# Mamba steps that take both channel halves at once: tiled gathers, 64-partition reads, and a step size summed on TensorE

## The chip, the cores and the metric

The kernel runs on one core of a Trainium2 chip. The metric is the device time of one launch in microseconds (us). The kernel before takes 8183.77 us, the median of three runs (8181.15 to 8186.65).

## The reference

Input is `x`, two images of 64 channels by 96 by 96 pixels, float32 throughout. Four layers follow each other.

```python
# layer 0: attention over the 9216 pixels of each image, then 1x1 conv, batch norm, residual
# layer 1: depthwise 3x1 and 1x3 + 1x1 conv + batch norm + relu, then one Mamba over the
#          9216 pixels of an image as ONE sequence, plus residual
# layer 2: four Mambas: forward and backward along the columns, then along the rows;
#          every row or column (96 long) is a sequence of its own
# layer 3: a dynamic 3x3 filter per channel group
def mamba(h):                                   # D_INNER = 128 channels d, 16 states s
    xm, z = split(h @ in_proj_w.T)
    xc = silu(causal_conv4(xm) + convd_b)
    dt, B, C = split(xc @ x_proj_w.T)           # 4, 16, 16
    dt = softplus(dt @ dt_proj_w.T + dt_proj_b) # per channel and pixel: the "step size"
    # for every channel d and state s, along the sequence t:
    #   hc = hc * exp(dt*A[d,s]) + dt * B[s] * xc[d];   y[d] = sum_s hc * C[s]
    return ((y + xc * Dp) * silu(z)) @ out_proj_w.T
```

The scan has 128 x 16 = 2048 independent rows (channel, state) for each pixel position, sixteen times the 128 partitions of the chip's memory.

## The kernel before, in words

Layer 0 (to about 2700 us of the profile) and layer 3 (the last 80 us) are not touched. The Mambas of layers 1 and 2 are run by the class `Mamba`, which is given a list of 120 *units*: 24 of layer 1 (`u.carry` is set: the scan goes on from the unit before), then 96 of layer 2 (`u.carry` is None). A unit is 768 pixels (`CH`), in two halves of 384 (`HALF`), and it takes 16 *steps*.

Per unit a prologue makes the channel values `xc`, the gate, the step size `dt` and the product `e = dt*xc`, each 128 channels by 768. `step_write` puts `dt` and `e`, together `u.both` of 128 x 1536, into a DRAM tile `rows` of 256 x 1536, twice, one copy under the other. Step n then reads 128 rows from row 8n on (`read`), so that partition p holds channel (p + 8n) mod 128; partition p always belongs to state p // 8. Over 16 steps each partition meets every channel that it has to. In layer 2 (`u.paired`) a step handles two such groups, 2m and 2m+1, over one half of the pixels, in two reads of 128 partitions by 3 KB; in layer 1 a step handles one group over all 768 pixels, in one read of 128 partitions by 6 KB.

A step is a chain over five engines: SyncE issues the read five steps ahead (`READ`); ScalarE makes exp(dt*A) three steps ahead (`decay`, L853 and L857); VectorE multiplies by B (`inputs`, L872 and L877, into a PSUM tile `place`) and scans (`scan`, L884 and L890); GpSimd multiplies the scanned `h` by C (L886 and L893); TensorE sums over the states with a permutation matrix of 128 x 128 (`gather`, L910), accumulating in a PSUM tile `low`. TensorE also makes B (`shared`, L866) and the prologue of later units (`mm`, L666; `conv`, L748 and L754).

The order is written out by hand: the table `PIECES` says at which step, counted from the unit's own first step, each prologue piece is issued, `lates` how many steps a gather lags its scan, and `run` issues all of it under a manual schedule, so every engine works through its queue in that order. SyncE issues every read and write of the steps, in one queue. The step size is log(1 + e^a) in parts: ScalarE writes `e`, `kept`, `log` and `dt`, and GpSimd adds them up in three full-width instructions (L805, L808, L811) before it multiplies by `xc` (L815).

Of the kernel before, what the change touches and what calls it, by code (L numbers as in the profile page):

```python
# [25 lines left out]
P = 128  # L26
# [497 lines left out]
def mamba_tables(k, pool):  # L524

    nc = k.nc
    G = P // 8
    t = SimpleNamespace()  # L530

    t.member = pool.tile([P, 8], FP, name="member")
    nc.vector.reduce_sum(t.member, k.ident.rearrange("p (g i) -> p i g", i=8), axis=AX.X)
    t.group = pool.tile([P, 2, G], FP, name="group")
    for j in range(2):
        nc.vector.reduce_sum(t.group[:, j], k.ident.rearrange("p (g i) -> p g i", i=8), axis=AX.X)

    t.turned = pool.tile([P, G, G], FP, name="turned")
    two = t.group.rearrange("p j g -> p (j g)")
    for n in range(G):  # L540
        nc.vector.tensor_copy(t.turned[:, n], two[:, G - n : 2 * G - n])

    pair = pool.tile([P, 2, P], FP, name="pair")
    nc.vector.tensor_copy(pair, k.ident.unsqueeze(1).to_broadcast([P, 2, P]))
    pair = pair.rearrange("p j c -> p (j c)")
    t.gather = [pair[:, P - 8 * n : 2 * P - 8 * n] for n in range(G)]

    t.centre = pool.tile([P, P], FP, name="centre")
    nc.vector.tensor_sub(t.centre, k.ident, k.mean_c)
    return t  # L550
# [8 lines left out]
def mamba_weights(k, w, pool, product, tables, i):  # L559
# [15 lines left out]
    p = product(tables.placed.rearrange("p s i -> p (s i)"), tables.group[:, 0], P, G)  # L575
# [38 lines left out]
class Mamba:  # L614
# [14 lines left out]

    STEPS = P // 8  # L630
# [3 lines left out]
    def __init__(self, k, tables, wk, dram, ps, ps_m):  # L634
        self.k, self.nc, self.t = k, k.nc, tables
        self.wk, self.dram, self.ps_m = wk, dram, ps_m


        self.places = [self.wide(ps.tile([P, 2 * NB], FP, name=f"place{i}")) for i in range(2)]
        self.low = [ps.tile([P, NB], FP, name=f"low{i}")[:, :HALF] for i in range(2)]  # L640
# [141 lines left out]
    def step_read(self, u):  # L782
# [3 lines left out]
        order = "p (j a t) -> p a j t" if u.paired else "p (a j t) -> p a j t"  # L786
        both = u.both.rearrange(order, a=2, j=2)
# [6 lines left out]
    def step_exp(self, u):  # L794
        nc = self.nc
        nc.scalar.activation(u.e, u.e, AF.Exp, scale=-1.0)
        nc.scalar.activation(u.kept, u.e, AF.Identity, bias=1.0)
        nc.scalar.activation(u.kept, u.kept, AF.Identity, bias=self.k.minus)  # L798
# [5 lines left out]
    def step_kept(self, u):  # L804
        self.nc.gpsimd.tensor_sub(u.kept, u.e, u.kept)  # L805

    def step_sum(self, u):
        self.nc.gpsimd.tensor_add(u.log, u.log, u.kept)  # L808

    def step_dt(self, u):  # L810
        self.nc.gpsimd.tensor_add(u.dt, u.dt, u.log)  # L811

    def step_u(self, u):
# [7 lines left out]
    def step_write(self, u):  # L821
        u.rows = self.dram.tile([2 * P, 2 * CH], FP, tag="rows", name="rows")
        for j in range(2):
            self.nc.sync.dma_start(out=u.rows[j * P : (j + 1) * P], in_=u.both)
# [10 lines left out]
    def paired(self, step):  # L835
        half, m = divmod(step, self.STEPS // 2)
        return half, (2 * m, 2 * m + 1)

    def read(self, u, step):
        u.dtu[step] = self.work("spread", 2 * CH, bufs=6)  # L840
        if not u.paired:
            self.nc.sync.dma_start(out=u.dtu[step], in_=u.rows[8 * step : 8 * step + P])
            return
        half, groups = self.paired(step)
        for q, n in enumerate(groups):
            row = u.rows[8 * n : 8 * n + P, bass.ts(half, CH)]
            self.nc.sync.dma_start(out=u.dtu[step][:, bass.ts(q, CH)], in_=row)

    def decay(self, u, step):

        h = u.h[step] = self.work("h", bufs=9)
        if not u.paired:
            self.nc.scalar.activation(h, u.dtu[step][:, :CH], AF.Exp, scale=u.w.rates[:, step : step + 1])  # L853
            return
        for q, n in enumerate(self.paired(step)[1]):
            dt = u.dtu[step][:, q * CH : q * CH + HALF]
            self.nc.scalar.activation(h[:, bass.ts(q, HALF)], dt, AF.Exp, scale=u.w.rates[:, n : n + 1])  # L857

    def shared(self, u, half=0):

        if u.paired:
            sides, halves = [self.low[0]], [half]
        else:
            (sides, u.B), halves = self.places[1], range(2)
        for j, p in zip(halves, sides):
            self.nc.tensor.matmul(p, lhsT=u.w.bc[0], rhs=u.xc[:, bass.ts(j, HALF)], start=True, stop=True)  # L866

    def inputs(self, u, step):

        if not u.paired:  # L870
            u.bx = self.places[0][1]
            self.nc.vector.tensor_mul(u.bx, u.dtu[step][:, CH:], u.B)  # L872
            return
        bx = self.places[step % 2][1].rearrange("p (q t) -> p q t", q=2)
        x = u.dtu[step].rearrange("p (q a t) -> p q a t", q=2, a=2)[:, :, 1]
        B = self.low[0].unsqueeze(1).to_broadcast([P, 2, HALF])
        self.nc.vector.tensor_mul(bx, x, B)  # L877

    def scan(self, u, step):
        nc = self.nc  # L880
        h = u.h[step]
        if not u.paired:
            first = u.carry[:, step : step + 1]
            nc.vector.tensor_tensor_scan(h, h, u.bx, first, ALU.mult, ALU.add)  # L884
            nc.gpsimd.tensor_copy(first, h[:, CH - 1 :])  # L885
            nc.gpsimd.tensor_mul(h, h, u.C)  # L886
            return
        bx = self.places[step % 2][1]
        way = slice(None, None, -1) if u.rev else slice(None)
        nc.vector.tensor_tensor_scan(h[:, way], h[:, way], bx[:, way], 0.0, ALU.mult, ALU.add)  # L890
        h = h.rearrange("p (q t) -> p q t", q=2)
        C = u.C[:, bass.ts(self.paired(step)[0], HALF)]
        nc.gpsimd.tensor_mul(h, h, C.unsqueeze(1).to_broadcast([P, 2, HALF]))  # L893

    def gather(self, u, step):

        if u.paired:
            half, groups = self.paired(step)
            parts = [(half, self.low[1], q, n) for q, n in enumerate(groups)]
            begin, end = step % 8 == 0, step % 8 == 7  # L900
        else:
            parts = [(j, p, j, step) for j, p in enumerate(self.low)]
            begin, end = step == 0, step == self.STEPS - 1
        h = u.h[step]
        if begin:
            for half, p in {half: p for half, p, _, _ in parts}.items():
                self.nc.tensor.matmul(p, lhsT=u.w.direct, rhs=u.xc[:, bass.ts(half, HALF)], start=True, stop=False)  # L907
        for i, (_, p, q, n) in enumerate(parts):
            stop = end and (i == 1 or not u.paired)
            self.nc.tensor.matmul(p, lhsT=self.t.gather[n], rhs=h[:, bass.ts(q, HALF)], start=False, stop=stop)  # L910

    def y_half(self, u):
        if u.paired:
            u.y = self.work("yg")
            self.nc.scalar.copy(u.y[:, :HALF], self.low[1])  # L915

    def y_read(self, u):
        if u.paired:
            self.nc.scalar.copy(u.y[:, HALF:], self.low[1])
        elif not u.drained:  # L920
            u.y = self.work("yg")
            for j, p in enumerate(self.low):
                self.nc.scalar.copy(u.y[:, bass.ts(j, HALF)], p)
# [20 lines left out]
    def tail_read(self, u):  # L944
# [25 lines left out]
        (-19, "step_read"),  # L970
        (-18, "step_exp"),
        (-17, "step_kept"),
        (-17, "step_log"),
        (-17, "c_mm"),
        (-15, "c_read"),
        (-15, "step_sum"),
        (-11, "step_dt"),
        (-9, "step_u"),
        (-8, "step_write"),
# [10 lines left out]
    def lates(now, s):  # L990
        halves = now and now[0].paired
        if s == 2 or (s == 10 and halves):
            return ()
        if s == 3 or (s == 11 and halves):
            return (3, 2)
        return (2,)

    def run(self, units, first, n_first, other):


        for u in units:
            u.dtu, u.h, u.paired, u.drained = {}, {}, not u.carry, False
        steps = [(u, s) for u in units for s in range(self.STEPS)]
        at = lambda n: steps[n] if 0 <= n < len(steps) else None
        reads = ("norm_square", "norm_root", "conv_read", "gate_read", "step_read", "c_read", "tail_read")

        table = [[] for _ in range(self.STEPS)]
        unit = lambda i: units[i] if i < len(units) else None
# [7 lines left out]
        for offset, name in self.PIECES:  # L1016
            if offset < 0:
# [3 lines left out]
                if name == "c_read":  # L1021
# [3 lines left out]
        for n in range(begin, len(steps) + end + 1):  # L1025
# [5 lines left out]
            if at(n):  # L1031
# [3 lines left out]
                if not u.paired:  # L1035
                    self.inputs(u, s)
                elif s % 2 == 0:
# [3 lines left out]
                if u.paired and s == 6:  # L1041
                    self.shared(u, 1)
                if s == (14 if u.paired else 15) and unit(n // self.STEPS + 1):
                    after = unit(n // self.STEPS + 1)
                    if after.paired and not u.paired:

                        for late in (2, 1, 0):
                            self.gather(u, s - late)
                        self.y_read(u)
                        u.drained = True  # L1050
                    self.shared(after)
            if n == -1:
                self.shared(units[0])

            for late in self.lates(at(n), s):
                if at(n - late) and not (at(n - late)[0].drained):
# [297 lines left out]
```

## Time and profile before

| what | value |
|---|---|
| median of three runs | 8183.77 us |
| the profiled execution: its time / its span | 8176.64 us / 8174.9 us |
| layer 1: first to last scan (L884) | 2753.5 to 3935.3 us, 384 steps |
| layer 2: first to last scan (L890) | 3944.0 to 8091.7 us, 1536 steps |
| span shares: TensorE, VectorE, ScalarE, GpSimd | 92, 83, 62, 58 % |
| DMA, bytes moved in the span | 1725.9 MB |

The profile is of one execution. Its page lists each engine's busy time, then the span in 40 slices, then the DMA queues, then the groups of instructions by line. The slices show two regimes: up to slice 14 (layer 0) the DMA engines are idle, and afterwards all five kinds of resource, DMA included, are busy at 60 to 98 per cent. A share over the whole span therefore says little; the stages have to be read by themselves. The trace records a float32 matmul as two instructions, so that one gather of a step (two matmuls) shows four.

### The profile page before, as it was taken

The numbers are of one execution on the slowest core, as the hardware profiler recorded it, in microseconds if no ns is written. First come the engines' busy times: TensorE is split into PE (matmuls) and PEld (weight loads), VectorE is DVE, ScalarE is ACT, GpSimd is POOL, SyncE is SP. The second block draws the span as 40 slices with busy tenths as digits, with TensorE's granted clock in tenths as the row PEclk, the third lists the DMA queues.
The fourth block names the chain that finished last, engine by engine and source line by source line (L and its number), as shares of the span: only waits on it lengthen the run. The fifth ranks groups of instructions, "written<-read, shape, count | busy, mean of one in ns | idle before, by whom it ended". The sixth has DMA issues, their size and how long they took to land.

```text
span 8174.9 us, 80364 instructions
## 1 busy us (share of the span) xinstructions
PE 7554.5 (92%) x24578; PEld 3358.0 (41%) x24578; DVE 6785.6 (83%) x5136; ACT 5045.4 (62%) x6473; POOL 4755.1 (58%) x3146
## 2 busy tenths in 40 slices
PE   9999999999999799999889998989999999999897
PEld 3333333333333344444444444444444444444443
DVE  6666666666666599988899999999999999999999
ACT  4444444444444566665676677777777777777774
POOL 0000000000000588888888888898999989888895
PEclk9999999999999798988999999999999999999999
DMA  1000000000000588777888888888898888888885
GB/s 42 1 1 1 1 1 1 3 4 4 4 4 5 205 294 296 284 286 277 292 315 317 317 321 333 330 324 331 334 337 328 330 336 336 331 321 334 324 329 211
DMA packets 538496, 1725.90 MB, mean 211 GB/s; under 512 B 59844, under 2 KB 60996, under 8 KB 537544
## 3 DMA queue, kind: packets, MB, share of 16 engines
q1 hardware_dynamic: 536608, 1717.66, 56.8%
q8 instruction: 194, 3.18, 0.2%
q10 hardware_dynamic: 1448, 3.05, 0.1%
q14 instruction: 246, 2.02, 0.1%
HBM read 1522.68 MB, written 197.79 MB: 210 GB/s over the span
## 4 chain that ended last, share of the span: by engine, by line
PE 21%; POOL 13%; issue 12%; ACT 8%; DMA 8%; DVE 4%; SPq 0%; DVEq 0%; ACTq 0%; POOLq 0%
PE low L910 10%; DMA spread<-rows 6%; POOL h L886 5%; POOL h L893 4%; PE mm L666 4%; ACT h L857 4%; PE conv L754 4%; DVE place L877 2%; DMA rows<-dtu 1%; PE low L907 1%; PE conv L748 1%; DVE h L890 1%; POOL dtu L811 1%; PE low L866 1%; ACT raw L773 1%
## 5 line engine op out<-in xcount | busy, mean ns | idle before, releaser
L910 PE MATMUL low<-h,pair 128*128 128x384 f32 x7680 | 2865.4, 515 | 44.2 <-POOL h L886 26.5
L893 POOL TENSOR_TENSOR h<-h,C 128x768 f32<-128x768 f32 x1536 | 2755.1, 1819 | 231.7 <-DVE h L890 225.1
L890 DVE TENSOR_TENSOR_SCAN h<-h,place 128x768 f32<-128x768 f32 x1536 | 2604.3, 1737 | 4.9 <-ACT h L857 4.9
L910 PEld LDWEIGHTS low<-h,pair 128*128 128x128 f32 x7680 | 1503.2, 201 | 1288.6 <-issue 270.7
L307 ACT ACTIVATE e<-f_exp 128x1536 f32<-128x1536 f32 x864 | 1207.1, 1449 | 1223.7 <-PE f_exp L297 1223.7
L363 DVE TENSOR_TENSOR acc_e<-acc_e,e 128x1536 f32<-128x1536 f32 x792 | 1389.9, 1755 | 684.5 <-ACT e L307 645.2
L857 ACT ACTIVATE h<-spread,xa 128x384 f32<-128x384 f32 x3072 | 1717.2, 607 | 368.7 <-DMA spread<-rows 336.8
L877 DVE TENSOR_TENSOR place<-spread,low 128x768 f32<-128x768 f32 x1536 | 1388.3, 949 | 251.0 <-PE low L866 238.4
L336 POOL TENSOR_TENSOR xa<-xa,t_att 64x512 f32<-64x512 f32 x36 | 45.4, 1261 | 2612.4 <-ACT t_att L334 2612.4
L314 PE MATMUL y_att<-e,xb 128*64 128x512 f32 x5184 | 1243.6, 601 | 0.0
L297 PE MATMUL f_exp<-theta,phi 64*128 64x512 f32 x5184 | 1234.4, 606 | 1.0 <-DVE xb L280 0.5
L297 PEld LDWEIGHTS f_exp<-theta,phi 64*128 64x128 f32 x5184 | 466.2, 186 | 754.6 <-issue 460.8
L884 DVE TENSOR_TENSOR_SCAN h<-h,state,place 128x768 f32<-128x768 f32 x384 | 696.1, 1813 | 67.7 <-ACT h L853 19.2
L886 POOL TENSOR_TENSOR h<-h,C 128x768 f32<-128x768 f32 x384 | 695.3, 1811 | 31.4 <-POOL state L885 1.0
L314 PEld LDWEIGHTS y_att<-e,xb 128*64 128x64 f32 x5184 | 341.5, 136 | 830.7 <-issue 829.3
L765 ACT ACTIVATE raw<-conv,cols 128x768 f32<-128x768 f32 x120 | 108.2, 901 | 886.1 <-PE conv L754 587.0
L754 PE MATMUL conv<-xn,xa 64*128 64x384 f32 (+3 forms) x1536 | 557.9, 503 | 16.6 <-DVE xa L1128 5.3
L872 DVE TENSOR_TENSOR place<-spread,place 128x768 f32<-128x768 f32 x384 | 369.1, 961 | 129.3 <-PE place L866 116.9
L853 ACT ACTIVATE h<-spread,rates 128x768 f32<-128x768 f32 x384 | 351.1, 931 | 175.0 <-DMA spread<-rows 173.6
L907 PE MATMUL low<-raw,xa 128*128 128x384 f32 x384 | 220.2, 662 | 257.8 <-ACT yg L915 175.6
L754 PEld LDWEIGHTS conv<-xn,xa 64*128 64x128 f32 x1536 | 277.6, 190 | 286.7 <-issue 98.7
L805 POOL TENSOR_TENSOR kept<-dtu,kept 128x768 f32<-128x768 f32 x120 | 218.2, 1819 | 285.1 <-ACT kept L798 285.1
(207 smaller groups left out, 6041.4 us busy)
## 6 DMA issues: line engine op xcount, KB each, us to landing
spread<-rows SPq DMA_DIRECT2D x3072, 384.0 KB, 6.4
spread<-rows SPq DMA_DIRECT2D x384, 768.0 KB, 4.5
rows<-dtu SPq DMA_DIRECT2D x240, 768.0 KB, 5.8
image<-pre SPq DMA_DIRECT2D x11, 384.0 KB, 2.3
xb<-image SPq DMA_DIRECT2D x11, 384.0 KB, 7.9
xa<-in_x SPq DMA_DIRECT2D x1, 2304.0 KB, 22.2
out<-xa ACTq DMA_DIRECT2D x7, 240.0 KB, 2.0
out<-xa SPq DMA_DIRECT2D x1, 1200.0 KB
```

Source lines behind the costliest of these rows:

```text
L297: nc.tensor.matmul(fs[j // 3][:, bass.ts(j % 3, NB)], lhsT=phi[at, bass.ts(m // 2, P)], rhs=theta[at, bass.ts(i, NB)], start=True, stop=True,)
L307: nc.scalar.activation(e, f, AF.Exp)
L314: nc.tensor.matmul(y[rows_of(m % 2)], lhsT=g[:, m, :], rhs=es[j // 3][:, bass.ts(j % 3, NB)], start=m < 2, stop=m >= KEYS - 2,)
L363: nc.vector.tensor_add(acc, acc, e)
L754: self.nc.tensor.matmul(p3[:, :, o], lhsT=lhsT, rhs=x3[:, :, i], **flags)
L857: self.nc.scalar.activation(h[:, bass.ts(q, HALF)], dt, AF.Exp, scale=u.w.rates[:, n : n + 1])
L877: self.nc.vector.tensor_mul(bx, x, B)
L884: nc.vector.tensor_tensor_scan(h, h, u.bx, first, ALU.mult, ALU.add)
L886: nc.gpsimd.tensor_mul(h, h, u.C)
L890: nc.vector.tensor_tensor_scan(h[:, way], h[:, way], bx[:, way], 0.0, ALU.mult, ALU.add)
L893: nc.gpsimd.tensor_mul(h, h, C.unsqueeze(1).to_broadcast([P, 2, HALF]))
L910: self.nc.tensor.matmul(p, lhsT=self.t.gather[n], rhs=h[:, bass.ts(q, HALF)], start=False, stop=stop)
```

## The change

A step now always takes one half of the pixels and, of both channel halves (channels 0 to 63 and 64 to 127), the group with the same number, its *turn* (0 to 7). This holds for both layers. The DRAM tile has each channel half twice, one copy under the other. Partition p holds channel 64q + (p + 8 turn) mod 64 for q = 0 and 1.

- Reads: two per step, as in layer 2 before, but each now fills 64 partitions with two pieces of 3 KB (both channel halves) instead of 128 partitions with one. Layer 1 had one read per step of 128 partitions by 6 KB.
- Writes: four of 64 partitions by 6 KB per unit instead of two of 128 by 6 KB.
- Gather: the permutation matrix is 128 x 64, and the two matmuls of a step write PSUM partitions 0 to 63 and 64 to 127 of one tile `y`.
- Layer 1: two exponentials and two scans of 384 per step instead of one of 768; two `place` tiles by turns; B and y one half at a time, as layer 2 has them.
- Layer 2's step size: the three GpSimd additions go; `dt_mm` adds the four parts in PSUM with identity matrices and `dt_read` copies the sum back on ScalarE. `c_mm`/`c_read` come two steps sooner, the product with `xc` and the write two steps sooner. Layer 1 keeps the GpSimd additions. `step_log` comes one step sooner in both layers.

```diff
 def mamba_tables(k, pool):
-    pair = pool.tile([P, 2, P], FP, name="pair")
-    nc.vector.tensor_copy(pair, k.ident.unsqueeze(1).to_broadcast([P, 2, P]))
+    pair = pool.tile([P, 2, C], FP, name="pair")
+    for j in range(2):
+        nc.vector.tensor_add(pair[:, j], k.ident[:, :C], k.ident[:, C:])
     pair = pair.rearrange("p j c -> p (j c)")
-    t.gather = [pair[:, P - 8 * n : 2 * P - 8 * n] for n in range(G)]
+    t.gather = [pair[:, C - 8 * n : 2 * C - 8 * n] for n in range(T)]
...
+    def dt_mm(self, u):
+        if not u.carry:
+            parts = (u.e, u.kept, u.log, u.dt)
+            u.p = self.mm([(self.k.ident, lambda j, part=part: part[:, j]) for part in parts])
+
+    def dt_read(self, u):
+        if not u.carry:
+            self.nc.scalar.copy(u.dt, self.by_half(u.p))
...
     def step_write(self, u):
         u.rows = self.dram.tile([2 * P, 2 * CH], FP, tag="rows", name="rows")
-        for j in range(2):
-            self.nc.sync.dma_start(out=u.rows[j * P : (j + 1) * P], in_=u.both)
+        for q in range(2):
+            for at in range(q * P, (q + 1) * P, C):
+                self.nc.sync.dma_start(out=u.rows[at : at + C], in_=u.both[rows_of(q)])
...
     def read(self, u, step):
+        half, turn = self.turn(step)
         u.dtu[step] = self.work("spread", 2 * CH, bufs=6)
-        if not u.paired:
-            self.nc.sync.dma_start(out=u.dtu[step], in_=u.rows[8 * step : 8 * step + P])
-            return
-        half, groups = self.paired(step)
-        for q, n in enumerate(groups):
-            row = u.rows[8 * n : 8 * n + P, bass.ts(half, CH)]
-            self.nc.sync.dma_start(out=u.dtu[step][:, bass.ts(q, CH)], in_=row)
+        rows = u.rows.rearrange("(q r) x -> r q x", q=2)[8 * turn : 8 * turn + C, :, bass.ts(half, CH)]
+        for j in range(2):
+            out = u.dtu[step][rows_of(j)].rearrange("p (q x) -> p q x", q=2)
+            self.nc.sync.dma_start(out=out, in_=rows)
...
     def scan(self, u, step):
+        if u.carry:
+            state = u.carry[:, 2 * turn : 2 * turn + 2]
+            for q in range(2):
+                at = bass.ts(q, HALF)
+                nc.vector.tensor_tensor_scan(h[:, at], h[:, at], bx[:, at], state[:, q : q + 1], ALU.mult, ALU.add)
+            nc.gpsimd.tensor_copy(state.unsqueeze(2), h2[:, :, HALF - 1 :])
+        else:
+            way = slice(None, None, -1) if u.rev else slice(None)
+            nc.vector.tensor_tensor_scan(h[:, way], h[:, way], bx[:, way], 0.0, ALU.mult, ALU.add)
...
     def gather(self, u, step):
+        half, turn = self.turn(step)
+        if turn == 0:
+            self.nc.tensor.matmul(self.y, lhsT=u.w.direct, rhs=u.xc[:, bass.ts(half, HALF)], start=True, stop=False)
+        for q in range(2):
+            rhs, stop = u.h[step][:, bass.ts(q, HALF)], turn == self.STEPS // 2 - 1
+            self.nc.tensor.matmul(self.y[rows_of(q)], lhsT=self.t.gather[turn], rhs=rhs, start=False, stop=stop)
...
     PIECES = (
         (-19, "step_read"),
+        (-19, "c_mm_2"),
         (-18, "step_exp"),
+        (-18, "step_log"),
         (-17, "step_kept"),
-        (-17, "step_log"),
-        (-17, "c_mm"),
-        (-15, "c_read"),
+        (-17, "c_read_2"),
+        (-17, "c_mm_1"),
+        (-17, "dt_mm"),
+        (-15, "c_read_1"),
+        (-15, "dt_read"),
         (-15, "step_sum"),
         (-11, "step_dt"),
-        (-9, "step_u"),
-        (-8, "step_write"),
+        (-11, "step_u_2"),
+        (-10, "write_2"),
+        (-9, "step_u_1"),
+        (-8, "write_1"),
```

A name that ends in `_1` acts in layer 1 alone, one that ends in `_2` (and `dt_mm`, `dt_read`) in layer 2 alone.

## The prediction

> **What bounds the kernel now.** I read the page first, the 40 slices before the shares.
>
> ```profile
> span 8174.9 us, 80364 instructions
> ...
> DMA  1000000000000588777888888888898888888885
> GB/s 42 1 1 1 1 1 1 3 4 4 4 4 5 205 294 296 284 286 277 292 315 317 317 321 333 330 324 331 334 337 328 330 336 336 331 321 334 324 329 211
> ...
> L910 PE MATMUL low<-h,pair 128*128 128x384 f32 x7680 | 2865.4, 515 | 44.2 <-POOL h L886 26.5
> L893 POOL TENSOR_TENSOR h<-h,C 128x768 f32<-128x768 f32 x1536 | 2755.1, 1819 | 231.7 <-DVE h L890 225.1
> L890 DVE TENSOR_TENSOR_SCAN h<-h,place 128x768 f32<-128x768 f32 x1536 | 2604.3, 1737 | 4.9 <-ACT h L857 4.9
> ...
> L877 DVE TENSOR_TENSOR place<-spread,low 128x768 f32<-128x768 f32 x1536 | 1388.3, 949 | 251.0 <-PE low L866 238.4
> ```
>
> The change acts from the first scan (2753 us) to the end of the last (8093 us), a stage of 5340 us with 1920 steps. There DMA runs at 0.7 to 0.9 all the time. The busy times by stretch, one in each layer, show how close the rivals for the bound are (columns: length, PE, PEld, DVE, ACT, POOL, clock, DMA share, GB/s).
>
> ```profile
> 3000.00:3800.00 800.00, 737.24 (x1904) 347.34 (x1902) 725.59 (x545) 502.93 (x581) 679.86 (x630) 0.91 0.78 285
> 5000.00:7500.00 2500.00, 2273.30 (x6297) 1162.68 (x6298) 2349.47 (x1866) 1828.40 (x2819) 2242.10 (x1312) 0.95 0.89 332
> ```
>
> The second has 933 scans, so 2.68 us per step and 42.9 us per unit, of which VectorE works 40.3, TensorE 39.0, DMA 38, GpSimd 38.5, ScalarE 31.4. VectorE is the bound: GpSimd waits for its scans, and its own loss is one wait (of that stretch: total, times, longest):
>
> ```profile
> DVE place L877 <- PE low L866: 141.8, 58, 4.3
> POOL h L893 <- DVE h L890: 108.4, 98, 2.2
> ```
>
> It waits for TensorE's B matmul, 2.4 us per unit, because that stands in the queue behind gathers which wait for GpSimd.
>
> **What the DMA does with 64 partitions.** The change halves the partitions of each read and write. The steps show no such transfer, but the start of the kernel does: L94 to L97 fill 64 partitions each, L94 and L95 by turns the lower and the upper half, 384 KB apiece as in the changed reads, and L98 fills 128. SyncE's queue, then the busy times by stretch of that start:
>
> ```profile
> 2.00 0.59 SPq L94 DMA_DIRECT2D xa<-in_x  x1
> 2.63 0.60 SPq L95 DMA_DIRECT2D xb<-in_x  x1
> 3.27 0.61 SPq L94 DMA_DIRECT2D xa<-in_x  x1
> 5.54 0.47 SPq L95 DMA_DIRECT2D xb<-in_x  x1
> ```
>
> ```profile
> 14.00:19.00 5.00, 4.85 (x38) 2.58 (x38) 4.96 (x36) 1.64 (x3) 0.00 (x0) 1.00 1.14 245
> 19.00:24.00 5.00, 5.00 (x58) 2.71 (x58) 3.02 (x9) 2.16 (x4) 0.00 (x0) 1.00 1.01 214
> 32.00:35.40 3.40, 3.40 (x36) 1.61 (x36) 1.55 (x5) 2.12 (x4) 0.00 (x0) 1.00 0.70 292
> 14.00:31.40 17.40, 17.25 (x174) 9.27 (x172) 12.36 (x55) 7.60 (x12) 0.00 (x0) 1.00 1.02 238
> ```
>
> Divide GB/s by the share for the rate of sixteen busy engines: with 128 partitions 292/0.70 = 417 GB/s; with 64, 214/1.01 = 212, and by turns over both halves 245/1.14 = 215. Over the whole half-partition stretch it is 238. Layer 2 now has 332/0.89 = 373. So the engines are all busy, but each at little over half speed.
>
> [...] layer 0 has the same shape of tile as the new gather (L314, 128*64, PSUM halves by turns); in the timeline of TensorE:
>
> ```profile
> 1001.38 2.85 PE L297 MATMUL f_exp<-theta,phi 64*128 64x512 f32 x12
> 1004.15 2.80 PE L314 MATMUL y_att<-e,xb 128*64 128x512 f32 x12
> 1006.88 2.85 PE L297 MATMUL f_exp<-theta,phi 64*128 64x512 f32 x12
> ...
> 6036.76 2.74 PE L910 MATMUL low<-h,pair 128*128 128x384 f32 x8
> 6039.34 0.81 PE L866 MATMUL low<-raw,xa 128*128 128x384 f32 x2
> ```
>
> Twelve tiled instructions of 512 columns take 2.73 us[...], 228 ns each; eight gathers of 384 take 2.58, 322 each.
>
> **The change part by part.**
>
> Gather: four instructions per step at 322 ns become four at 228 x 384/512 = 171 ns: 1.29 to 0.68 us, 9.7 us per unit less on TensorE. No bound engine.
>
> Step size in layer 2: GpSimd loses three of 1.82 us, 5.5 per unit. TensorE gains eight matmuls, 16 x 322 ns = 5.2 us, ScalarE a copy of 0.78 (as L831). TensorE ends at 34.5 us per unit, GpSimd at 33.0, ScalarE at 32.1, all below VectorE's unchanged 40.3. `dt_mm` waits for ScalarE's four parts; behind it in TensorE's queue stand the gathers, and behind those the y copy. [...] that can delay them by up to 5 us once per unit, bounded by 9 `h` buffers against a lag of two steps; I take nothing, with 0 to 2 us per unit as bounds.
>
> Moved pieces: `c_mm`, `c_read`, `step_log` move within TensorE's and ScalarE's queues past at most two steps, cost nothing while those have slack (8 and 10 us per unit), and otherwise at most their own 0.8 to 1.3 us per unit. The write moves on SyncE ahead of two steps' reads. It waits for GpSimd's product, as L824 does now; the reads queued behind it wait too, with 5 steps of lead. `u.both` has one buffer, so ScalarE's next `step_read`, seven steps after the write instead of five, waits until it has landed; the exponentials stand behind it. Now that takes 5.8 us, and the cover is 19; with a slow queue of five steps in front it takes about 20, and the cover is 26.
>
> Layer 1: two scans for one. From 949 ns for 768 columns and 677 for 512 (L877, L330) a VectorE instruction has an estimated fixed part of 133 ns, so 16 x 0.13 = 2.1 us per unit on top of 44.7. ScalarE pays 2 x 607 - 931 = 283 ns per step, 4.5 us on 31. SyncE issues a second read. Against it, two `place` tiles remove layer 1's wait for B.
>
> Reads and writes: the bytes stay, 2 x 393,216 per step and 1,572,864 per unit written, 884,736 per step in all. What changes is the rate. I take 238 GB/s, the whole half-partition stretch, which holds both same-half and mixed moments: 3.72 us per step, more than VectorE's 2.52. **This term decides.** The lower bound is 211 GB/s (4.19 us); the upper 280[...] (3.16 us). That the rate stays 373 (2.37 us, hidden) is the main rival. Four writes for two add SyncE issue time (0.3 us each), hidden beside transfers of 1.8 us.
>
> Sum: 1920 x 3.72 = 7142 us for 5340, that is +1802. The profiled execution took 8176.6 (span 8174.9 and 1.7 around it), which makes 9979; the median of the runs lies 7 us above the profiled time, so 9985. The gains on TensorE and GpSimd bring nothing then, because every engine waits for the reads.
>
> **The rivals.**
>
> 1. [...] For it: six transfers at the start are a short trial. Against it: they alternated too and reached only 215. Then VectorE stays the bound and loses its wait: 2.4 us x 96 units = 233 in layer 2, and some 49.3 - 47.4 = 1.9 us x 24 = 45 in layer 1. That gives 8177 - 278 + 7 = 7905, **faster**. It decides when the mixed rate exceeds 884,736 / 2.7 us = 328 GB/s.
>
> 2. [...] 280 to 310 GB/s, 3.16 to 2.85 us per step: 8910 to 8320.
>
> 3. [...] TensorE then has 39.0 + 5.2 = 44.2 us per unit and, at 42.9 now, becomes the bound: at least 1.3 x 96 = 125 us, 8310, if the DMA does not bind. Layer 0's rows speak against it.
>
> **How the numbers follow.** A difference of 0.2 per cent is about what a measurement of this kernel can tell. DMA bound at 211 to 280 GB/s: 0.66, own range 8910 to 10900. Rivals 2 and 3: 0.10. Gain and loss cancel within 0.2 per cent: 0.02. Rival 1: 0.22, of which I put 0.09 above 7950, since a part of the waits may stay. The point is that of the first case, 9985. A range from 7950 to 10900 leaves out 0.13 below and about 0.05 above. Faster 0.22, same 0.02, slower 0.76.
>
> **What would show it.** Right: in layer 2 the DMA share is near 1.0 while GB/s falls to 210 to 280; exponentials and `inputs` wait for `spread<-rows` for about 1 us in every step; time to landing of a read rises from 6.4 us to over 10; VectorE is busy under 75 per cent; the gather group's busy time falls by some 40 per cent all the same. Wrong: reads landing in 6 to 8 us at over 330 GB/s, and VectorE at 97 per cent. TensorE near 100 per cent would speak for rival 3.

## The result and the profile after

The changed kernel takes 9523.06 us (median of 4 runs, 9512.79 to 9545.77) against 8185.21 for the kernel before in the same session: the ratio is 1.1636, with a 95% interval of 1.1613 to 1.166. It is slower by 1338 us. The profiled execution took 9521.7 us.

The page of the changed kernel, first the slices of DMA, then the chain that ended last:

```profile
span 9519.8 us, 85326 instructions
...
DMA  1000000000069999999999999999999999999997
GB/s 36 1 1 1 1 1 4 4 4 4 6 149 261 245 254 249 260 244 244 259 250 253 246 253 260 246 252 253 265 254 251 260 259 267 255 257 265 258 253 171
...
DMA 47%; PE 7%; ACT 5%; issue 2%; SPq 2%; DVE 2%; POOL 2%; ACTq 0%; DVEq 0%; POOLq 0%
...
L932 POOL TENSOR_TENSOR h<-h,C 128x768 f32<-128x768 f32 x1920 | 3452.7, 1812 | 2003.9 <-DVE h L931 1942.3
L916 DVE TENSOR_TENSOR place<-spread,B 128x768 f32<-128x768 f32 x1920 | 1782.1, 953 | 1526.8 <-DMA spread<-rows 855.4
...
L931 DVE TENSOR_TENSOR_SCAN h<-h,place 128x768 f32<-128x768 f32 x1536 | 2621.2, 1740 | 159.1 <-ACT h L906 152.9
...
L941 PE MATMUL y<-h,pair 128*64 128x384 f32 x7680 | 1735.5, 578 | 9.9 <-POOL h L932 9.9
```

The DMA row stands at 9 from the first step to the last, while the GB/s row has fallen from about 330 to about 255. Almost half of the chain is DMA. Most of the idle time before VectorE's input product (L916) is now ended by reads, where it had been TensorE's B. The gathers (L941) did become cheap, 1735.5 us of busy time for 2865.4 before, and it did not help. The busy times by stretch say the same (columns as before: length, PE, PEld, DVE, ACT, POOL, clock, DMA share, GB/s), and the waits of the second stretch, ahead of its DMA issues:

```profile
3000.00:3800.00 800.00, 620.48 (x1683) 214.37 (x1681) 626.93 (x708) 489.62 (x739) 592.47 (x554) 0.76 1.03 250
5000.00:7500.00 2500.00, 1794.61 (x5556) 712.10 (x5556) 1838.94 (x1437) 1437.34 (x2193) 1493.26 (x874) 0.81 1.03 254
```

```profile
ACT h L906 <- DMA spread<-rows: 830.6, 400, 7.6
DVE place L916 <- DMA spread<-rows: 363.6, 226, 4.0
...
DVE place L916 <- PE B L910: 212.4, 64, 5.9
```

```profile
spread<-rows SPq DMA_DIRECT2D x1431, 384.0 KB, 12.7
rows<-dtu SPq DMA_DIRECT2D x180, 384.0 KB, 9.6
```

716 scans in 2500 us are 3.49 us per step; before it was 2.68. The bytes of a step have not changed: 884,736 B at 254 GB/s are 3.48 us, so the rate is what sets the step. No other resource is over 74 per cent busy.

### The profile page after: what moved, and what is told of

Its sections match the earlier page's. It is cut to its first block, busy times and chain, and to the rows that moved or that the text cites. A ratio compares the mean times of both kernels' runs of the same rounds, so it can differ in the third digit from the quotient of the medians.

```text
span 9519.8 us, 85326 instructions
## 1 busy us (share of the span) xinstructions
PE 7530.7 (79%) x26114; PEld 2795.8 (29%) x26114; DVE 6823.3 (72%) x5523; ACT 5192.1 (55%) x6953; POOL 4252.7 (45%) x2858
## 4 chain that ended last, share of the span: by engine, by line
DMA 47%; PE 7%; ACT 5%; issue 2%; SPq 2%; DVE 2%; POOL 2%; ACTq 0%; DVEq 0%; POOLq 0%
DMA spread<-rows 46%; PE mm L671 4%; ACT h L906 2%; SPq L897 2%; PE y L941 1%; DMA rows<-dtu 1%; POOL h L932 1%; PE conv L759 1%; DVE xa L1270 1%; DVE place L916 1%; PE y L938 0%; PE B L910 0%; ACT dtu L796 0%; ACT dtu L795 0%; DVE h L931 0%
## 5 line engine op out<-in xcount | busy, mean ns | idle before, releaser
L916 DVE TENSOR_TENSOR place<-spread,B 128x768 f32<-128x768 f32 x1920 | 1782.1, 953 | 1526.8 <-DMA spread<-rows 855.4
L941 PE MATMUL y<-h,pair 128*64 128x384 f32 x7680 | 1735.5, 578 | 9.9 <-POOL h L932 9.9
L941 PEld LDWEIGHTS y<-h,pair 128*64 128x64 f32 x7680 | 526.4, 155 | 1089.7 <-issue 872.5
L927 DVE TENSOR_TENSOR_SCAN h<-h,state,place 128x384 f32<-128x384 f32 x768 | 716.8, 995 | 28.8 <-POOL state L928 11.6
L938 PE MATMUL y<-raw,xa 128*128 128x384 f32 x384 | 222.3, 668 | 630.7 <-ACT yg L945 545.0
L906 ACT ACTIVATE h<-spread,rates 128x384 f32<-128x384 f32 x768 | 428.8, 607 | 434.8 <-DMA spread<-rows 383.1
L671 PE MATMUL mm<-dtu,ident 128*128 128x384 f32 x768 | 365.5, 585 | 295.9 <-ACT C L883 295.9
L671 PE MATMUL mm<-xn,mats 64*128 64x384 f32 x480 | 280.9, 724 | 320.0 <-ACT raw L770 320.0
L671 PE MATMUL mm<-raw,xa 128*128 128x384 f32 x768 | 326.3, 551 | 117.2 <-ACT dtu L796 117.1
L671 PE MATMUL mm<-yg,xa 128*64 128x384 f32 x384 | 242.3, 778 | 209.6 <-ACT raw L777 208.4
```

The source lines that it names most:

```text
L671: self.nc.tensor.matmul(o, lhsT=lhsT, rhs=x, start=n == 0, stop=n == len(terms) - 1)
L916: self.nc.vector.tensor_mul(bx, x, self.B.unsqueeze(1).to_broadcast([P, 2, HALF]))
L927: nc.vector.tensor_tensor_scan(h[:, at], h[:, at], bx[:, at], state[:, q : q + 1], ALU.mult, ALU.add)
L941: self.nc.tensor.matmul(self.y[rows_of(q)], lhsT=self.t.gather[turn], rhs=rhs, start=False, stop=stop)
```

## The experiments

In all, twelve kernels ran. Their times are medians against the kernel before on the same chip. A gap below is the mean time from one scan's start to the next in layer 2, by the step's place in its unit, from the scans' start times in the trace. The *second stretch* is the one from 5000 to 7500 us. In the diffs, lines left out are marked by three dots.

### The reads alone, and the reads taken back (e3, e1)

```diff
 # e3: the kernel before
-            row = u.rows[8 * n : 8 * n + P, bass.ts(half, CH)]
-            self.nc.sync.dma_start(out=u.dtu[step][:, bass.ts(q, CH)], in_=row)
...
+            two = bass.AP(one.tensor, one.offset, [[row, C], [8 * row, 2], list(last)])
+            out = u.dtu[step][rows_of(j)].rearrange("p (q x) -> p q x", q=2)
+            self.nc.sync.dma_start(out=out, in_=two)
```

For each partition half j, `two` names the rows from 8n + 64j on, for both groups n. In layer 1 the one read of 128 partitions by 6 KB becomes two of 64.

> The kernel before with one thing changed: every read is cut by partitions, two transfers of 64 partitions with two pieces of 3 KB (in layer 1 one of 6 KB) instead of two of 128 by 3 KB (layer 1: one of 128 by 6 KB). The two transfers read different rows. Theory P: the rate falls to the 254 GB/s of the changed kernel, 884,736 B per step take 3.48 us, 1920 steps 6690 us instead of 5340: 9530 us, the whole of the loss. Theory A: no row is read twice at once: 8190. Theory O: 8190.

Measured: 9394.09 us, ratio 1.1492 (1.1467 to 1.1517). With nothing changed but the partitions of a read (and, in layer 1, two transfers for one), a loss of 1210 us appears, where the whole change loses 1338. Theory A falls with it, since here the two transfers read different rows.

```profile
3000.00:3800.00 800.00, 657.91 (x1654) 312.45 (x1654) 630.36 (x470) 445.88 (x507) 588.40 (x546) 0.89 1.01 247
5000.00:7500.00 2500.00, 1956.81 (x5125) 988.48 (x5124) 1942.41 (x1520) 1501.43 (x2281) 1821.30 (x1063) 0.88 1.03 268
```

Again a full DMA, at 268 GB/s instead of 332 in layer 2 and at 247 instead of 285 in layer 1. In layer 1 a partition still gets one piece of 6 KB, so the two pieces of layer 2's reads are not needed for the loss.

```diff
 # e1: the changed kernel
-        rows = u.rows.rearrange("(q r) x -> r q x", q=2)[8 * turn : 8 * turn + C, :, bass.ts(half, CH)]
-        for j in range(2):
-            out = u.dtu[step][rows_of(j)].rearrange("p (q x) -> p q x", q=2)
-            self.nc.sync.dma_start(out=out, in_=rows)
+        for q in range(2):
+            rows = u.rows[q * C + 8 * turn : q * C + 8 * turn + P, bass.ts(half, CH)]
+            self.nc.sync.dma_start(out=u.dtu[step][:, bass.ts(q, CH)], in_=rows)
```

> The changed kernel, with each step's two reads of 64 partitions by two pieces put back to two reads of 128 partitions by one piece: the same bytes and the same number of transfers. The rows are those of other channels (the second channel half is read from row 64 + 8 turn on), so a step computes the scan of other channels than the reference asks for; no duration depends on that. Theory P (a transfer of 64 partitions runs at little over half the rate): the reads go back to about 373 GB/s, 884,736 B per step take 2.4 us and are hidden, VectorE is the bound: 7905 us, 7850 to 8100. Theory A (the same DRAM rows are read twice by two transfers): half of the rows are still read twice, so some 8800. Theory O (the order, the y tile or layer 1's two scans cost the time): 9500, as with the change.

Measured: 8828.94 us, ratio 1.0789 (1.0763 to 1.0815). All three expectations missed except, by its number, theory A's, which e3 refutes. The reads land in 6.2 us again, and the DMA is no longer full:

```profile
5000.00:7500.00 2500.00, 1861.73 (x6186) 752.87 (x6186) 2029.10 (x1597) 1564.72 (x2452) 1662.70 (x974) 0.86 0.84 283
```

But nothing else is full either. So the change holds a second loss, which the reads had covered. In layer 1 the step is 3.06 us, as good as before (3.10); in layer 2 it is 3.13. The gaps find the place: step 12 comes 6.54 us after step 11, where the kernel before has 3.35, and step 13 another 3.34 later (1.70). That other channels are read does not show in the engines' times: the mean VectorE instruction of the stretch takes 1.27 us, 1.28 in the changed kernel, and the mean GpSimd instruction 1.71 in both.

### The write that came two steps sooner (e7, e9)

Step 12's read is the first that stands behind layer 2's write in SyncE's queue. e7 is e1 with one entry of the table put back:

```diff
-        (-10, "write_2"),
         (-9, "step_u_1"),
+        (-8, "write_2"),
         (-8, "write_1"),
```

> e1 (reads of 128 partitions, same bytes, of other channels) with the write of layer 2 put back from ten to eight steps ahead; the PSUM sum stays. In e1's layer 2 the scan of step 12 comes 6.5 us after that of step 11 where 3.35 us are the least (both kernels' even steps), and step 12's read is the first one that stands behind the write in SyncE's queue. Theory W (the earlier write holds up the reads behind it, since it waits for GpSimd's product): the gap goes, 96 x 3.2 = 300 us less, 8520. Theory T (TensorE's sum makes the gap, wherever the write is): it stays or moves, 8800 to 8850.

Measured: 8217.11 us, ratio 1.0036 (1.0024 to 1.0047): 612 us less than e1, twice what theory W expected. The gap before step 12 is 3.35 again, and theory W counted that one alone; the one before step 13 fell from 3.34 to 1.73 as well, and the one at the border between units from 7.15 to 5.41. SyncE's timeline shows one write in e1, then one in e7:

```profile
6071.58 5.40 SPq L896 DMA_DIRECT2D spread<-rows  x5
6083.71 4.28 SPq L876 DMA_DIRECT2D rows<-dtu  x4
6088.40 11.01 SPq L896 DMA_DIRECT2D spread<-rows  x13
```

```profile
5994.06 11.17 SPq L896 DMA_DIRECT2D spread<-rows  x10
6007.55 4.77 SPq L876 DMA_DIRECT2D rows<-dtu  x4
6012.43 36.09 SPq L896 DMA_DIRECT2D spread<-rows  x32
```

In e1 the last read is issued at 6076.98 (6071.58 + 5.40). SyncE then waits 6.7 us for GpSimd's product and takes 4.3 us for four issues: 11.4 us pass without a read, in which the five steps of lead run out. In e7 it is 7.2 us. Over the second stretch this pause has a mean of 11.3 us in e1 and 7.1 in e7; the kernel before bears one of 9.0. The same edit on the changed kernel itself:

> The changed kernel, computing everything, with the write of layer 2 at eight steps ahead instead of ten; reads of 64 partitions stay. With reads of 128 partitions (e1 to e7) that edit was worth 612 us. Theory of one bound: the reads of 64 partitions hide it, 9400 to 9530 us. Theory of a sum: 9523 - 612 = 8910.

It is e7's edit, on the change.

Measured: 9199.59 us, ratio 1.1256 (1.1223 to 1.1288). Neither theory holds. The edit gains 323 us with reads of 64 partitions, 612 with 128. It is worth half as much, and the reads remain the bound, but it isn't hidden altogether: the rate itself rises to 270 GB/s, at the same DMA share of 1.03.

```profile
5000.00:7500.00 2500.00, 1855.94 (x5898) 740.78 (x5896) 1941.95 (x1526) 1533.52 (x2335) 1582.39 (x928) 0.86 1.03 270
```

The gap before step 12 falls from 8.51 to 3.81 us, while the one before step 14, whose read is now the first behind the write, rises from 3.79 to 5.94. Read the other way, 128 partitions gain 694 us with the write at ten steps and 982 with it at eight. And e3, which has the reads of 64 partitions and the write at eight steps but nothing else of the change, is 194 us slower than e9. So the loss of 1338 us is not 1210 and a small rest: the moved write adds 323, and the other parts take about 194 back.

### The step size back on GpSimd (e5)

The edit makes layer 2 take layer 1's path in the pieces from `step_exp` to `c_read_2`.

> The changed kernel with the step size of layer 2 put back: three GpSimd additions, C, the product with xc and the write at the steps that layer 1 and the kernel before use. Reads of 64 partitions and tiled gathers stay. Theory of one bound (a step takes as long as its reads, everything else is hidden): 3.48 us per step stay, 9450 to 9550 us. Theory of a sum (the PSUM sum costs its 350 us on top, as it did in the kernel before, 8537 against 8184): 9170.

Measured: 9377.48 us, ratio 1.1453 (1.1397 to 1.1508), 146 us under the changed kernel and between the two theories, nearer that of one bound. It moves the write to eight steps as well, so e9 is its fair neighbour: with the write equal, the sum in PSUM is 178 us faster than GpSimd's (9200 against 9377).

### How long an engine stays in one half (e8, e10)

The changed kernel moves 254 GB/s where one half alone moved 212 at the kernel's start. e8 puts two steps' lower halves together, then both upper ones; e10 cuts each read by channel half and takes the partition halves by turns. By an estimate, the 384 KB of a read shared evenly by the 16 engines of the page, an engine then has 48 or 12 KB in a row for one half, where the change has 24. The *theory of drift* of the two expectations is my guess, from 212 and 254, that shorter turns raise the rate. In e8, `read_half` is the read of one partition half.

```diff
 # e8
-            if at(n + self.READ):
-                self.read(*at(n + self.READ))
+            if at(n + 4) and n % 2 == 0:
+                self.read(*at(n + 4))
...
-        for j in range(2):
+        for j in range(2):
+            for s in (step, step + 1):
+                self.read_half(u, s, j)
```

```diff
 # e10
-        for j in range(2):
-            out = u.dtu[step][rows_of(j)].rearrange("p (q x) -> p q x", q=2)
-            self.nc.sync.dma_start(out=out, in_=rows)
+        for q in range(2):
+            for j in range(2):
+                self.nc.sync.dma_start(out=u.dtu[step][rows_of(j), bass.ts(q, CH)], in_=rows[:, q])
```

> The changed kernel, computing everything, with the reads of two steps put together: both lower halves first, then both upper halves (four transfers every second step, four to five steps ahead). Each engine then has 48 KB for one half in a row instead of 24. Theory of drift [...] 215 to 235 GB/s, 884,736 B per step take 3.8 to 4.1 us, 10050 to 10700 us. If the rate does not depend on the order of the halves: 254 GB/s, 9450 to 9600.

Measured: 10032.65 us, ratio 1.2231 (1.22 to 1.2262), 3.73 us per step.

> The changed kernel, computing everything, with each read of 64 partitions cut in two by channel half, and the partition halves by turns: four transfers of 192 KB per step, so that an engine has 12 KB for one half in a row instead of 24 (and 48 in e8). Theory of drift: the rate goes on rising as it did from 236 GB/s (e8) to 254, to some 270 to 300, 3.28 to 2.95 us per step, 8500 to 9140 us. If 24 KB is already as mixed as it gets, or if the number of transfers[...] takes over: 9500 or more.

Measured: 9304.12 us, ratio 1.137 (1.1339 to 1.14). The second stretch of e8, then of e10:

```profile
5000.00:7500.00 2500.00, 1691.41 (x5181) 666.11 (x5180) 1721.28 (x1344) 1337.27 (x2042) 1393.38 (x815) 0.80 1.04 236
```

```profile
5000.00:7500.00 2500.00, 1828.50 (x5769) 726.86 (x5770) 1908.41 (x1493) 1519.80 (x2286) 1554.55 (x911) 0.82 1.02 264
```

With 48, 24 and 12 KB the rate is 236, 254 and 264 GB/s at a full DMA: the finer the turns, the higher, as the theory of drift has it. The last step is smaller than the first and smaller than expected. The writes account for the unevenness. By the trace's packet records, the rate in the times with no write in flight is 224, 243 and 262 GB/s, two even steps; in the times with a write in flight e10 moved 279 GB/s in all, the changed kernel 332. e10's write packets took longer (345 ns per 6144 B on average, against 275 in the changed kernel). Why shorter turns are faster was not shown: the records do not name the engine.

### What the other parts are worth (e4, e6, e12)

e4 is the kernel before with the change's pieces from `step_exp` to `c_read_2` and its table.

> The kernel before with the step size of layer 2 alone changed: summed in PSUM, C two steps sooner, the write two steps sooner; gathers, reads and layer 1 as before. The prediction's own sums give TensorE 39.0 + 5.2 = 44.2 us per unit of layer 2 against 42.9 for a unit now, so TensorE becomes the bound: 96 x 1.3 = 125 us more, 8310, or more with the new waits. The opposite theory: what counts is that GpSimd gets 5.5 us per unit back and gathers stop waiting for it; then VectorE's wait for B goes and it is 7950 to 8100.

Measured: 8536.9 us, ratio 1.0433 (1.0413 to 1.0453). TensorE holds the steps up, as the prediction's third rival reckoned for gathers that cost what they did before (44.2 us per unit), but the loss is 353 us, not 125. TensorE works 93 per cent of the second stretch, 91 before. It is not full: the sum stands in its queue as one block of 16 instructions, and the gaps stretch where B is due, 7.48 us at the unit's border and 5.38 before step 8 (5.38 and 3.91 in the kernel before). VectorE's wait for B is 307.4 us in the second stretch, for 141.8 before:

```profile
DVE place L924 <- PE low L913: 307.4, 99, 5.7
```

e4 has the write at ten steps too. The gap before step 12 stays at 3.35 us, though, and the exponentials wait only 5.2 us in the whole stretch for reads, so the trace does not put the loss there.

e6 is e1 with e5's edit.

> Reads of 128 partitions with the bytes of the change (of other channels, as in e1: the outputs are those of other channels) and the step size summed on GpSimd at the steps of before; what is left of the change is the tiled gather, layer 1's new steps and the four writes of 64 partitions. If the prediction's rival 1 was right about the gather (VectorE loses its wait for B once TensorE has 29 us per unit instead of 39): 7950 to 8100 us. If the tiled gather brings nothing off the bound: 8150 to 8250. If the sum in PSUM is not what separates e1 from the kernel before: 8800, as e1.

Measured: 8434.43 us, ratio 1.0296 (1.0278 to 1.0313); no expectation was right. The waits of SyncE in the second stretch:

```profile
SPq L896 <- DVE place L915: 562.4, 224, 3.7
SPq L876 <- POOL dtu L870: 447.8, 54, 9.1
```

With the sum on GpSimd the product comes late, and SyncE waits 8.3 us for it per write. The kernel before waits as long (461.6 us in 58 waits), but then issues two writes of 128 partitions, at a median of 0.32 us; a write of 64 partitions has a median of 0.48 in the changed kernel and 0.97 in e7, and there are four. The gap is where those writes stand, 8.0 us after step 13. The pause without a read is 12.8 us, for 9.0 in the kernel before and 7.1 in e7. The writes of 64 partitions also took longer in transfer (435 ns per packet for 299), and no run here separates that from their issue. Against e6, then, the sum in PSUM has a use of its own: in e7 SyncE waits 2.3 us per write for the product instead of 8.3.

```diff
 # e12: e7 with
-        for q in range(2):
-            for at in range(q * P, (q + 1) * P, C):
-                self.nc.sync.dma_start(out=u.rows[at : at + C], in_=u.both[rows_of(q)])
+        for j in range(2):
+            self.nc.sync.dma_start(out=u.rows[j * P : (j + 1) * P], in_=u.both)
```

> e7 (reads of 128 partitions with the bytes of the change, of other channels; the write at eight steps ahead; tiled gather and PSUM sum as in the change) with the writes put back to two of 128 partitions: no transfer of 64 partitions is left in the steps, and the transfers are those of the kernel before. What is left of the change is the tiled gather, the PSUM sum of layer 2 and layer 1's new steps. Theory W (e7's writes of 64 partitions, 385 ns per packet against 299 before, and four issues for two, hold back the reads behind them): 7950 to 8100 us, most of the prediction's rival 1. Theory E (the border between units holds e7: TensorE's sum waits for ScalarE, and B and y stand behind it): 8180 to 8220 us, as e7.

Measured: 8131.0 us, ratio 0.9945 (0.9933 to 0.9957), the only kernel of the study that is faster than the kernel before, by 48 us or half a per cent. It reads other channels, so it is a measure of what the design could be worth and not a version to use. The gain is all in layer 1, 2.89 us per step for 3.10 (82 us); layer 2 has 2.716 for 2.702. Against e7, the writes of 128 partitions bring 70 us in layer 1 (from 3.07 us per step) and 26 in layer 2: theory W has a part in layer 1, and theory E holds for layer 2. TensorE's timeline at a unit's border:

```profile
6031.80 0.81 PE L908 MATMUL B<-raw,xa 128*128 128x384 f32 x2
6032.54 1.51 PE L939 MATMUL y<-h,pair 128*64 128x384 f32 x8
6037.06 1.65 PE L671 MATMUL mm<-dtu,ident 128*128 128x384 f32 x2 [3.00 <-ACT C L882]
...
6043.11 0.81 PE L671 MATMUL mm<-dtu,ident 128*128 128x384 f32 x2
6043.85 1.51 PE L939 MATMUL y<-h,pair 128*64 128x384 f32 x8
```

The sum waits 3.0 us until ScalarE has read C out of the one PSUM buffer that all `mm` share. Then it holds TensorE for 6.8 us, and from 6034 to 6043.85 no gather runs. VectorE's wait for B is what it was:

```profile
DVE place L914 <- PE B L908: 136.6, 96, 3.2
```

141.8 us in the kernel before, over 58 waits of up to 4.3; now 96 shorter ones.

### Two versions with all rows right (e2, e11)

To have 128-partition reads and the tiled gather together, each channel half must lie in three copies.

```diff
 # e2
+        u.rows = self.dram.tile([6 * C, 2 * CH], FP, tag="rows", name="rows")
...
+            for at in range(3 * C * q, 3 * C * (q + 1), C):
+                n = min(C, 3 * C * (q + 1) - 8 - at)
+                self.nc.sync.dma_start(out=u.rows[at : at + n], in_=u.both[q * C : q * C + n])
...
+            at = 3 * C * q + 8 * turn
+            self.nc.sync.dma_start(out=u.dtu[step][:, bass.ts(q, CH)], in_=u.rows[at : at + P, bass.ts(half, CH)])
 # e11, besides the table of e7
+            out = u.rows[3 * C * q : 3 * C * (q + 1)].rearrange("(c r) x -> r c x", c=3)
+            self.nc.sync.dma_start(out=out, in_=u.both[rows_of(q)].unsqueeze(1).to_broadcast([C, 3, 2 * CH]))
```

> The changed kernel, computing everything: each channel half is written 184 rows deep (three copies, the last cut) in six transfers per unit instead of four, so that a read of one channel half fills 128 partitions again. Per step 786,432 B are read and 141,312 written, 927,744 in all. Theory P: at 373 GB/s that is 2.49 us per step, just under VectorE's 2.52, so a little waiting is left: 7900 to 8100 us, faster than both kernels. Theory A: also fast, since no row is read by two transfers at once. Theory O: 9500.

Measured: 9333.9 us, ratio 1.14 (1.1377 to 1.1424). The expectation missed by over 1200 us. The reason stands in SyncE's timeline:

```profile
5997.49 38.19 SPq L897 DMA_DIRECT2D spread<-rows  x32
6042.68 8.11 SPq L877 DMA_DIRECT2D rows<-dtu  x6
6050.90 9.29 SPq L897 DMA_DIRECT2D spread<-rows  x11
```

Seven us of waiting and 8.1 us of issuing six writes, 15.2 us without a read; step 12 comes 10.45 us after step 11.

> e2 (computes everything, reads of 128 partitions from three copies) with two writes per unit instead of six, each writing all three copies of a channel half from 64 partitions, and at eight steps ahead in layer 2. It is e7 with the right rows and 943,718 B per step instead of 884,736. If the 96 per cent DMA share of e7 (327 GB/s, so 341 at full) is a limit: 2.77 us per step, 1920 x 2.77 = 5320 for 5340, 8150 to 8250, no better than the kernel before. If the DMA runs at the 373 GB/s of the kernel before: 2.53 us, hidden by VectorE, and fewer writes free SyncE: 8000 to 8100.

Measured: 8589.26 us, ratio 1.05 (1.0474 to 1.0526), better than e2 by 745 us, with two writes for six and the write at eight steps for ten, which no run separates, and still slower than both expectations. The DMA is at 0.97 with 321 GB/s, and the writes from 64 partitions take 417 ns per packet of 6144 B on average, against 299 from 128 in the kernel before. Of the versions that read the right rows, none beat the kernel before.

## Why the prediction was right, point by point

**The deciding term** was right in kind, and its size was off on the safe side. The step was 884,736 B at 238 GB/s, 3.72 us; it measured 254 GB/s and 3.48 us over the stage (2753 to 9438 us). The mis-sized term is the rate: 238 was the mean of a start with long transfers into one half, and e8 and e10 show that shorter turns raise it (236 and 264 GB/s). e8, whose turns are twice as long as the change's, moved 236 GB/s and took 10,033 us, about the time that was forecast. The stage of the changed kernel is 1345 us longer (6685 for 5340) instead of 1802.

**Its marks** came, all but a part of one: DMA share 1.03 at 254 GB/s; the exponentials wait 830.6 / 716 = 1.16 us per step for reads, `inputs` only 363.6 / 716 = 0.51, where about 1 us was named for both; landing 12.7 us; VectorE at 74 per cent; the gathers' busy time down by 39 per cent.

**The gather's price** held. In e12's TensorE timeline eight of them take 1.35 us up to the next start, 169 ns each; 171 was forecast.

```profile
6017.07 1.51 PE L939 MATMUL y<-h,pair 128*64 128x384 f32 x8
6018.42 1.45 PE L671 MATMUL mm<-yg,xa 128*64 128x384 f32 x4
```

**The moved write was costed at nothing, and that step failed.** The cover named was five steps of reads. In the second stretch of the changed kernel SyncE pauses 3.8 us before the writes of a unit and then takes 4.1 us over four issues, not the 1.2 that I took from writes of 128 partitions. The place of the write is worth 323 us inside the changed kernel (e9) and 612 without its reads (e7). That the reads behind it lose their lead is shown for e1. In the changed kernel the pause without a read is 8.7 us, for 7.2 in e9 and 9.0 in the kernel before, so there the pause alone does not explain the 323 us.

**A part of the closeness is luck.** The rate was set too low and the moved write left out, and the two errors work against each other. With the write at eight steps the reads ran at 270 GB/s, not 238, and the time was 9200 us: still inside the range, but 785 us under the point instead of 462.

**The sum in PSUM was costed at nothing**, with 0 to 2 us per unit as bounds. Against GpSimd's sum it is a gain (e9 against e5, 178 us; e7 against e6, 217), given the tiled gather; without it, a loss of 353 us (e4, with the write at ten steps).

**Rival 1**, a rate that does not fall, was priced at 7905 us. With every transfer of 64 partitions gone, e12 gives 8131. Layer 1 gained 82 us, more than the 45 priced (its 47.4 us per unit does not follow from 44.7 + 2.1 = 46.8, which would have made it 60); layer 2's 233 us, VectorE's wait for B, did not come. I had said that this wait comes from gathers that wait for GpSimd. In e12 GpSimd is busy 77 per cent of the second stretch, for 90 before, and the wait is still there. In the timeline shown, the gathers now stand behind pieces that wait for ScalarE; that B is late for the same reason was not tested alone. Rival 2, a rate between, came in part, but stayed short of its 280 GB/s (my estimate, close to half of the bytes at 212 and half at 417): 254 is a fifth of the way from one half's 212 to the 417 of full transfers. Rival 3, gathers at the price of before, did not come about, as the 169 ns show.

What stays open: why the rate went from 254 to 270 GB/s when only the write moved (e9). By the packet records of the second stretch, both parts of the rate rose: from 243 to 255 GB/s in the times with no write in flight, and from 332 to 362 with one. No empty queue shows in the trace while SyncE waits: over sixty units of layer 2, the changed kernel's mean DMA share is 0.99 in the lowest of a unit's 16 gaps. No run here tells more.

## What to carry to other kernels

Price a transfer by the partitions that it fills as well as by its bytes (e3: 268 GB/s for 332 with the same bytes): look in the kernel's own trace for one of the same shape, even in a stage that has nothing to do with the change, and divide GB/s by the DMA share. A bound that is lifted uncovers the next, so undo a change's parts in more than one order: here the same edit of one line was worth 323 or 612 us. Look at what stands behind a transfer that waits in its queue: in e1 and e2 the reads behind a waiting write came too late, after 11.4 and 15.2 us without a read, and the write's issue time counted once for each piece into which it was cut (4.3 us for four, 8.1 for six).

## What the runs showed of the hardware

Issue time on SyncE differed with the shape. A read of 64 partitions in two pieces took 573 ns at the least and in the median of the changed kernel; one of 128 in one piece took 319 at the least, with medians of 371 (kernel before) to 429 (e1). Writes from 64 partitions had medians of 484 (changed kernel) to 1354 ns (e2), those from 128 of 320 (kernel before) and 400 (e12).

In the second stretch, writes from 64 partitions took 245 to 345 ns per packet of 6144 B while the reads had 64 too (e9, e10), and 385 to 435 beside reads of 128 (e7, e1). While such a write was in flight e1 moved 216 GB/s in all; with writes from 128 partitions the kernel before moved 327.

In four runs TensorE's granted clock was lower where TensorE was busy less of the second stretch: 0.98 at 93 per cent (e4), 0.95 at 91 (kernel before), 0.81 at 72 (changed kernel), 0.79 at 65 (e5). Since TensorE was not the bound in the changed kernel, no run here prices that.
